# Selective scans beside other stages: work issued by its TensorE time, sums on four column tiles, wider rows of parts

## The chip, the cores and the metric

The kernel runs on one core of one Trainium2 chip. The metric is the device time of one execution in microseconds (us). The engines are named as in the profile: PE (TensorE), DVE (VectorE), ACT (ScalarE), POOL (GpSimd) and SP, the queue that issues nearly all DMAs.

## The reference

Four images of 96 channels and 64 x 64 pixels (L = 4096) pass through four residual layers, each on the group-normalised image (32 groups). All is float32.

```
layer 0: attention pooling: softmax over 4096 keys for 1024 queries, 3 heads of 32,
         a 3x3 neighbourhood softmax, a 5x5 depthwise convolution, a projection
layer 1: in_proj to 2 x 192 channels, 3x3 depthwise conv, silu, selective scan in four directions,
         layer norm, gate, 1x1 conv to 384, 3x3 depthwise conv, 1x1 conv to 96, squeeze-excite
layer 2: a dense 3x3 convolution
layer 3: 1x1 convs, two 3x3 depthwise branches, a selective scan like that of layer 1 (with D * u
         in place of layer 1's + D), layer norms, gates, squeeze convs, a channel softmax, a projection
scan, for each image, direction k, channel d (192) and state n (16), over 4096 positions t:
   delta = softplus(dt);  h[t] = exp(-delta[t] * A[d, n]) * h[t-1] + delta[t] * u[t] * B[n, t]
   y[t] = sum over n of h[t] * C[n, t]
directions: rows forward, rows backward, columns forward, columns backward; the four y are added
```

Layer 1's reference writes its recurrence as a ratio of cumulative sums; the kernel computes it as the recurrence above.

## The kernel before

A scan of one image in one layer is cut into 32 **groups**: four directions, four chunks of `CH` = 1024 positions, two halves of 96 channels. A group has `NG` = 12 **units**; a unit holds 8 channels x 16 states on 128 partitions and 1024 positions. Eight scans (`SCANS`: layer 1 of images 0 and 1, layer 3 of 0 and 1, then the same for images 2 and 3) make 3072 units, issued one after the other by `unit(i, ...)`.

What one unit does, by function:

- `fetch` (SP): a DMA spreads 8 rows of delta (`dd`, in DRAM) over 128 partitions into `rep`, 512 KB, four units ahead (`AHEAD`); `rep` has 10 buffers.
- `decays` (ACT): exp of `rep` times the decay rate, in place.
- `drive` (PE): two bf16 matmuls of 512 columns spread delta * u, which `prepare` cut into three bf16 parts (`parts`), over the 16 states into `bx`, a PSUM tile of two buffers.
- `times_b` (DVE): `bx` times B. `scan` (DVE): the recurrence as one instruction into `hs` (three buffers). `carry_on` (ACT) keeps the last column for the next chunk.
- `times_c` (POOL): `hs` times C, back into `rep`.
- `collect` (PE), every third unit: six float32 matmuls with 32 columns of weights (`addn`) add the 16 states of three units on three column tiles of the accumulator `acc` (PSUM, one buffer). `place` deals out the units so that each of the three tiles collects 32 channels in a row: rows 0 to 95 of `acc`.
- `output`, once a group: adds `acc` to `yo` or copies it (DVE or ACT), and SP stores it into `y_row` or `y_col` in DRAM, 96 rows. Backward directions first load what the forward ones left.

`prepare(g)` computes delta, delta * u, B and C of a group two groups ahead: a generator, advanced a step at a time in the slot `prep`. It writes du into DRAM and reads it back into `parts` by four DMAs of 24 partitions x 6 x 512 bf16 values.

**The other stages** run in the same stream. `first(b)` is layer 0 and the start of layer 1, `second(b)` the end of layer 1 to the start of layer 3's scan, `third(b)` the end of layer 3 and `last(b)` the same for the last image; `BESIDE` says which runs beside which scan (the last scan has `third` three times and `last`). `first(0)` runs ahead of the scans, alone. Each is a generator: it yields None after a matmul that something must evacuate, a number where only other engines have work, and a tuple inside a long accumulation. `Slots.begin` advances it up to such a point, `Slots.end` runs the evacuation.

Scheduling is by hand (`manual_schedule`): each engine runs its instructions in the order in which Python issues them. In `unit` the order was

```
first_.begin | decays(i+2) | scan(i) | carry_on(i-1) | times_c(i) | collect(j) | drive(i+2)
  | first_.end, rest.begin (if over 0.9 of the budget is left) | times_b(i+1) | output | first_.end, rest.end
```

where `first_` is a slot of work (or of `prep` in its first steps) and `rest` a second one. The budget is counted in yields: each matmul of a convolution is 1, an evacuated one 1, a number itself. A unit is given 3.5, 3.7 or 3.2 of it (`PACE`, by stage), less 2.1 where a `collect` is due, and what is left over is passed on (up to 0.5).

The names in profile lines: `one` and `held` are PSUM tiles of the other stages, `band`, `upad`, `vpad`, `hp` their padded images, `V` their working image, `ex` the attention's exponentials. All matmuls have one line, that of the helper `mm` (L949).

Of the kernel before, what the change touches and what calls it, by code (L numbers as in the profile page):

```python
# [18 lines left out]
L = H * W  # L19
# [21 lines left out]
PHI_EPS = 1e-12  # L41

# [101 lines left out]
def _constants(i):  # L144
    c = {}
    c["ident"] = np.eye(128, dtype=np.float32)
    g = np.zeros((128, 96), np.float32)
    for j in range(96):
        g[j // 3 * 3 : j // 3 * 3 + 3, j] = 1.0 / 3.0
    c["group"] = g  # L150
    c["ones"] = np.ones((128, 96), np.float32)
    c["mean1"] = np.full((128, 96), 1.0 / 96.0, np.float32)
    c["mean2"] = np.full((128, 96), 1.0 / 192.0, np.float32)


    s = np.zeros((128, 56), np.float32)
    s[np.arange(128), 24 + np.arange(128) % 8] = 1.0
    c["addn"] = s

    s = np.zeros((128, 2, 15), np.float32)  # L160
    s[:, 0, 7], s[:, 1, 7] = 1.0 / 96.0, 1.0 / 192.0
    c["means"] = s

    s = np.arange(34)[:, None] - np.arange(W)[None, :] // 2
    s = np.tile((s >= 0) & (s <= 2), (3, 2)).astype(np.float32)
    c["near"] = np.concatenate([s, np.zeros((26, 128), np.float32)])
    c["heads"] = np.kron(np.eye(4, dtype=np.float32), np.ones((32, 32), np.float32))

    s = np.zeros((2, 64, 4, E), np.float32)
    for tag, w in (("l1_", i["L1_conv_dt_proj_w"]), ("l3_", i["L3_conv_ss_dt_w"])):  # L170
        s[:, DTROW[tag] : DTROW[tag] + R] = w.transpose(2, 0, 1)
    c["dtw2"] = s.reshape(128, 4, E)

    for tag, w in (("l1_", i["L1_conv_A_log"]), ("l3_", i["L3_conv_ss_Alog"])):
        c[tag + "alogn"] = w.reshape(4, E // 8, 8, N).transpose(3, 2, 0, 1).reshape(128, 4, E // 8)

    s = np.zeros((4, 32, 4, N, 8), np.float32)
    for q in range(4):
        for d in range(8):
            s[q, 3 * d : 3 * d + 3, q, :, d] = 1.0  # L180
    c["spread"] = s.reshape(128, 4, 128)
    return c
# [712 lines left out]
def streams(ctx: ExitStack, tc: tile.TileContext, x, wts, cst, out, wat, cat, flag):  # L895
# [51 lines left out]

    def mm(o, lhsT, rhs, first=True, last=True):
        nc.tensor.matmul(o, lhsT=lhsT, rhs=rhs, start=first, stop=last)  # L949
# [58 lines left out]
    with tc.tile_pool(name="start", bufs=1) as T:  # L1008
# [9 lines left out]
        for tag in ("l1_", "l3_"):  # L1018
            decay[tag] = keep.tile([128, 4, E // 8], F32, name=tag + "decay")
            n, m, shape = cat[tag + "alogn"]  # L1020
            src = _view(t0, (n - n2, m, shape))
            if tag == "l3_":
                nc.scalar.activation(decay[tag], src, AF.Exp)
                src = decay[tag]
            nc.vector.tensor_scalar(decay[tag], src, -1.0, None, ALU.mult)
            dsum[tag] = derived(2)
            nc.vector.tensor_reduce(dsum[tag], wv(tag + "d"), AX.X, ALU.add)


    def image(name):  # L1030
        return [dram.tile([96, L], F32, name=f"{name}{b}") for b in range(B)]

    res1, res2, gate1, skip3, gate3 = (image(k) for k in ("res1_", "res2_", "gate1_", "skip3_", "gate3_"))
    u_row, u_col, y_row, y_col = ([image(f"{k}{h}_") for h in range(2)] for k in ("urow", "ucol", "yrow", "ycol"))
# [384 lines left out]
    def directions(pool, b, tag):  # L1419

        V = pool.tile([96, 2, L], F32, name="V", bufs=1)
        with tc.tile_pool(name="dirs", bufs=1) as T:
            full = len(groups) // len(SCANS) * (SCANS.index((tag, b)) + 1)
            cols = []
            for h in range(2):
                while stored[0] < full - 1 + h:
                    yield WAIT
                t = T.tile([96, W, H], F32, name="yc", bufs=2)
                cols.append(t)
                for j in range(4):  # L1430
                    nc.sync.dma_start(out=t.rearrange("p a b -> p (a b)")[:, bass.ts(j, CH)],
                                      in_=y_col[h][b][:, bass.ts(j, CH)])
                    nc.sync.dma_start(out=V[:, h, bass.ts(j, CH)], in_=y_row[h][b][:, bass.ts(j, CH)])
                yield 4
# [198 lines left out]
    def last(b):  # L1633

        with tc.tile_pool(name="p3x", bufs=1) as PX:
# [5 lines left out]
            with tc.tile_pool(name="turn", bufs=1) as T:  # L1641
                for h in range(2):
                    t = T.tile([96, W, H], F32, name="yc")
                    for j in range(4):
                        nc.sync.dma_start(out=t.rearrange("p a b -> p (a b)")[:, bass.ts(j, CH)],
                                          in_=y_col[h][b][:, bass.ts(j, CH)])
# [7 lines left out]
    def finish(PX, b, V, blocks):  # L1654

        with tc.tile_pool(name="p3", bufs=2) as pool:
# [25 lines left out]
            def loaded(name, src, bufs):  # L1682
                def load(j):
                    t = pool.tile([96, PCH], F32, tag=name, name=name, bufs=bufs)
                    nc.sync.dma_start(out=t, in_=src[b][:, bass.ts(j, PCH)])
# [126 lines left out]
    carry = keep.tile([128, 2, NG], F32, name="carry")  # L1812
    sums = keep.tile([96, len(SCANS), 4, 2, 2 * NCH], F32, name="sums")
    cuts = [keep.tile([128, 6, PCH], BF16, name=f"parts{n}") for n in range(2)]
# [24 lines left out]
    def prepare(g):  # L1839
# [83 lines left out]
        def to_parts():  # L1923
            for q in range(4):
                nc.sync.dma_start(
                    out=parts[32 * q : 32 * q + 24],
                    in_=du[:, :, bass.ts(q % 2, PCH)].rearrange("(s m d) r x -> m (d r) s x", m=2, d=8)[q // 2])
# [6 lines left out]
    def place(i):  # L1934
# [3 lines left out]
        return g, m % 3 * 4 + m // 3  # L1938

    def fetch(i):  # L1940

        g, m = place(i)
        rep = sp.tile([128, CH], F32, name="rep", bufs=10)
# [10 lines left out]
    def drive(i):  # L1954
# [4 lines left out]
        for e in range(2):  # L1959
            mm(bx[:, bass.ts(e, PCH)], spread[:, 2 * (m % 2) + e, :], parts[:, m // 2, :])  # L1960
# [25 lines left out]
    def collect(i):  # L1986
# [3 lines left out]
        if m == 0:  # L1990
            live["acc"] = ps.tile([128, CH], F32, tag="acc", name="acc", bufs=1)
            live["yo"] = sp.tile([96, CH], F32, name="yo", bufs=1)
            if back:
                nc.sync.dma_start(out=live["yo"], in_=(y_row if axis == "r" else y_col)[h][b][:, natural(c, back)])
            elif axis == "r" and tag == "l3_":
                nc.sync.dma_start(out=live["yo"], in_=u_row[h][b][:, natural(c, back)])
        hs = [live.pop(i + q)[0] for q in range(3)]
        w = addn[:, 24 - 8 * (m // 3) : 56 - 8 * (m // 3)]
        for e in range(2):
            for q in range(3):  # L2000
                mm(live["acc"][bass.ts(q, 32), bass.ts(e, PCH)], w, hs[q][:, bass.ts(e, PCH)], m == 0, m == NG - 3)

    def output(i):
# [4 lines left out]
        yo = live["yo"]  # L2008
        ya = time(live["acc"][:96], back, 0, CH)
# [13 lines left out]
    PACE = {"first": 3.5, "second": 3.7, "third": 3.2}  # L2023
# [15 lines left out]
    def unit(i, prep, work, budget):  # L2039
# [8 lines left out]
        j = i - BEHIND - 2  # L2048
        due = j >= 0 and j % 3 == 0
        first_, rest = (prep, work) if 1 <= prep.slots <= 3 else (work, idle)  # L2050
        budget -= first_.begin(budget)
# [5 lines left out]
        times_c(i)  # L2057
        if due:
# [3 lines left out]
        if first_ is work and budget > 0.9:  # L2062
            rest = work
        if rest is not idle:
            first_.end()
            budget -= rest.begin(budget)
        if i + 1 < total:
            times_b(i + 1)
        if due and j % NG == NG - 3:
            store.append(output(j))  # L2070
        first_.end()
        rest.end()
        if first_ is not prep:
            prep.begin(0)
            prep.end()
        return budget

    class Slots:
# [5 lines left out]
        def begin(self, budget):  # L2084

            if budget < 0:
                return 0
            self.slots += 1
            used = 0
            v = next(self.stage, 0)  # L2090
            if v == WAIT:
                return budget
            while isinstance(v, tuple):
                used += v[0]
                if used >= budget:
                    return used
                v = next(self.stage, 0)
            self.open = v is None
            return used + (1 if self.open else v)
# [19 lines left out]
    with tc.manual_schedule():  # L2119
# [15 lines left out]
        for i in range(total):  # L2135
# [11 lines left out]
            owed = min(owed, 0.5) + PACE[BESIDE[s][0][0]] - (2.1 if i % 3 == 1 else 0.0)  # L2147
            owed = unit(i, prep, work, owed)
        for j in range(total - 3, total, 3):
# [54 lines left out]
```

## Time and profile before

| | |
|---|---|
| three runs, median (lowest to highest) | 14,391.75 us (14,391.1 to 14,398.4) |
| the profiled execution, its own time | 14,400.5 us |
| its span, first to last instruction | 14,398.6 us |
| mean granted PE clock | 0.866 |
| PE / DVE / POOL / ACT busy | 84 / 81 / 71 / 61% |
| DMA: moved, mean rate | 2,644 MB, 184 GB/s |
| ahead of the first scan instruction | 690 us |
| the eight scans | 1632, 1656, 1666, 1633, 1630, 1659, 1668, 2036 us |
| after the last scan instruction | 129 us |

Busy shares are means over stages. In a group's line, the number after xcount is the busy time in us, then the mean duration in ns, then the idle time of the engine just ahead of it and what ended most of that. A waits line reads: who <- for whom: us in total, times, longest. float32 matmuls leave two records each.

### The profile page before, as it was taken

What the parts mean: (1) busy time and instruction counts of PE and PEld (TensorE: products, weight loads), DVE (VectorE), ACT (ScalarE), POOL (GpSimd) and SP (SyncE); (2) the same over time, 40 slices, a digit from 0 to 9 for tenths busy, and PEclk for the clock granted to TensorE, in tenths of its full rate; (3) what the DMA queues carried; (4) which work ended last, traced back from release to release, by engine and by line L of the source; (5) the groups of instructions that cost most, each with busy time, mean ns of one, the idle gap of its engine ahead of it and who ended that gap; (6) DMA issues with size and microseconds to landing.
All of it is one profiled execution on the core that took longest, in us unless ns stands there. A gap on an engine that the chain in (4) does not pass through costs nothing. (4 is left out here: it accounts for less than half of the span.)

```text
span 14398.6 us, 127507 instructions
## 1 busy us (share of the span) xinstructions
PE 12060.6 (84%) x40149; PEld 3562.9 (25%) x40802; DVE 11655.5 (81%) x7509; ACT 8713.8 (61%) x12340; POOL 10204.6 (71%) x4636
## 2 busy tenths in 40 slices
PE   8888887988889797889878887988979887777776
PEld 2322321322223222222222222222313222111111
DVE  1488898888878888889888898888888888778776
ACT  3266575557756676665766566566756667665554
POOL 0177886877868777778877787777868778666564
PEclk9889997998889897989879898898979888777777
DMA  0277787787877878778877788787877878677674
GB/s 9 64 174 179 193 216 198 187 207 187 223 178 199 205 200 209 180 174 206 223 185 178 186 209 219 176 207 186 212 186 197 209 190 220 168 179 173 161 184 111
DMA packets 902736, 2644.48 MB, mean 184 GB/s; under 512 B 107104, under 2 KB 257088, under 8 KB 902048
## 3 DMA queue, kind: packets, MB, share of 16 engines
q1 hardware_dynamic: 901392, 2634.72, 73.2%
q8 instruction: 324, 5.31, 0.2%
q14 instruction: 364, 2.98, 0.1%
q10 hardware_dynamic: 656, 1.46, 0.0%
HBM read 2169.16 MB, written 466.62 MB: 183 GB/s over the span
## 5 line engine op out<-in xcount | busy, mean ns | idle before, releaser
L1984 POOL TENSOR_TENSOR rep<-hs,bc 128x1024 f32<-128x1024 f32 x3072 | 7221.1, 2356 | 3057.2 <-DVE hs L1972 2499.8
L1972 DVE TENSOR_TENSOR_SCAN hs<-rep,carry,bx 128x1024 f32<-128x1024 f32 x2304 | 5401.7, 2344 | 266.0 <-ACT carry L1980 12.2
L1965 DVE TENSOR_TENSOR bx<-bx,bc 128x1024 f32<-128x1024 f32 x3072 | 3723.7, 1212 | 852.5 <-PE bx L949 432.9
L1952 ACT ACTIVATE rep<-rep,l_decay 128x1024 f32<-128x1024 f32 x3072 | 3495.7, 1143 | 519.9 <-DMA rep<-dd 502.7
L949 PE MATMUL bx<-parts,spread 128*128 128x512 bf16 x5491 | 1938.0, 429 | 1589.5 <-DVE hs L1972 1522.7
L949 PE MATMUL acc<-rep,ct 128*32 128x512 f32 x12288 | 2439.7, 703 | 16.0 <-POOL rep L1984 11.2
L1972 DVE TENSOR_TENSOR_SCAN hs<-rep,bx 128x1024 f32<-128x1024 f32 x768 | 1754.6, 2285 | 139.0 <-ACT carry L1980 47.8
L949 PEld LDWEIGHTS <-spread 128*128 128x128 bf16 x6144 | 426.0, 100 | 4080.5 <-DVE hs L1972 2610.9
L949 PE MATMUL one<-band,dg 96*96 96x512 f32 x2304 | 1048.0, 592 | 4.0
L949 PE MATMUL one<-upad,diag 96*96 96x512 f32 x2016 | 949.2, 607 | 3.8
L949 PEld LDWEIGHTS acc<-rep,ct 128*32 128x32 f32 x12288 | 492.2, 123 | 1676.0 <-issue 1401.2
L949 PE MATMUL one<-qq,kk 96*128 96x512 f32 x1152 | 684.4, 678 | 114.4 <-ACT ex L1288 75.2
L1288 ACT ACTIVATE ex<-one 128x512 f32<-128x512 f32 x576 | 342.4, 594 | 580.4 <-PE one L949 573.9
L949 PE MATMUL one<-pr,ct 6*96 6x512 f32 x1024 | 621.3, 690 | 78.6 <-DVE V L1193 10.4
L1952 ACT ACT_TABLE_LOAD x495 | 635.1, 1283 | 80.5 <-DMA rep<-dd 72.3
L949 PE MATMUL one<-hp,diag 96*96 96x512 f32 x1152 | 578.2, 642 | 31.3 <-POOL diag L1113 28.6
L1980 ACT COPY carry<-hs 128x1 f32<-128x1 f32 x2304 | 408.7, 177 | 287.0 <-DVE hs L1972 285.4
L949 PE MATMUL one<-vpad,diag 96*96 96x512 f32 x1200 | 559.2, 601 | 1.9
L949 PE MATMUL held<-ex,cols 128*32 128x256 f32 x3072 | 518.8, 415 | 8.0 <-ACT ex L1288 1.2
L949 PE MATMUL held<-ex,vT 128*32 128x256 f32 x3072 | 519.1, 415 | 0.0
L949 PEld LDWEIGHTS one<-band,dg 96*96 96x96 f32 x2304 | 374.6, 163 | 489.8 <-issue 423.7
L949 PEld LDWEIGHTS one<-upad,diag 96*96 96x96 f32 x2016 | 336.7, 167 | 438.9 <-issue 378.2
(3421 smaller groups left out, 14154.2 us busy)
## 6 DMA issues: line engine op xcount, KB each, us to landing
rep<-dd SPq DMA_DIRECT2D x3072, 512.0 KB
parts<-du SPq DMA_DIRECT2D x1024, 144.0 KB
bc<-rows SPq DMA_DIRECT2D x256, 512.0 KB
dd<-delta SPq DMA_DIRECT2D x256, 384.0 KB
du<-cut SPq DMA_DIRECT2D x256, 384.0 KB
us<-urow SPq DMA_DIRECT2D x128, 384.0 KB
du<-cut SPq DMA_DIRECT2D x256, 192.0 KB
yrow<-yo SPq DMA_DIRECT2D x128, 384.0 KB
```

Of the source, the lines that this page charges most:

```text
L949: nc.tensor.matmul(o, lhsT=lhsT, rhs=rhs, start=first, stop=last)
L1288: nc.scalar.activation(last.rearrange("p a b -> p (a b)"), p, AF.Exp, scale=HD**-0.5)
L1952: nc.scalar.activation(a, a, AF.Exp, scale=decay[tag][:, k, NG * h + m : NG * h + m + 1])
L1965: nc.vector.tensor_mul(bx, bx, ready[i // NG][2][:, 0, :])
L1972: nc.vector.tensor_tensor_scan(out=hs, data0=a, data1=bx, initial=carry[:, h, m : m + 1] if c else 0.0, op0=ALU.mult, op1=ALU.add)
L1980: nc.scalar.copy(carry[:, h, m : m + 1], live[i][1][:, CH - 1 : CH])
L1984: nc.gpsimd.tensor_tensor(a, hs, ready[i // NG][2][:, 1, :], ALU.mult)
```

## The change

1. **Issue by PE time.** `mm` adds up an estimate of PE time (`spent`: columns x passes / 2400; bf16 one pass, float32 four, 32-column tiles 1.07, the two-tile product of `prepare` two). A unit is given `PACE[s]` us (2.95 to 3.45 by scan), less `DRIVE` 0.43 and, where a `collect` is due, `SUM` 1.71; up to 0.6 is passed on. A step without matmul counts `SLOT` 0.5 per number.
2. **Order in the unit.** Work is issued in up to three portions: ahead of the scan, ahead of `collect` and `drive`, and after `drive`. `times_b(i+1)` moves up to just after `times_c(i)`; all evacuations come after it.
3. **Four units a sum.** `collect` takes four units on four column tiles, one unit later (`BEHIND - 3`); `place` is `m % 4 * 3 + m // 4`. Each 32 partitions of `acc` hold 24 channels and a gap of 8, so `yo`, `y_row` and `y_col` have 128 rows, `yo` is one lasting tile, the sum of D (`dsum`) comes from a constant in that layout, and the other stages read y without the gaps by four DMAs of 24 rows each (`ungapped`).
4. **Parts** are [128, 3, 1024]: four DMAs of 24 partitions x 3 x 1024 values, rows of 2048 bytes; `drive` picks one of four row blocks and half of the columns.
5. `rep` has 12 buffers[...].

The diff, cut to its core:

```
+PACE = (2.95,3.45,3.45,2.95,2.95,3.45,3.45,3.2)
...
     def mm(o, lhsT, rhs, first=True, last=True):
+        n = 1
+        for d in rhs.shape[1:]:
+            n *= d
+        m = o.shape[0]
+        passes = 1 if rhs.dtype == BF16 else 1.07 if m == 32 else 2 if m == R + 2 * N else 4
+        spent[0] += n * passes / 2400
...
+    def ungapped(dst, src, cols):
+        for q in range(4):
+            nc.sync.dma_start(out=dst[24 * q : 24 * q + 24], in_=src[32 * q : 32 * q + 24, cols])
...
-                    nc.sync.dma_start(out=t.rearrange("p a b -> p (a b)")[:, bass.ts(j, CH)],
-                                      in_=y_col[h][b][:, bass.ts(j, CH)])
-                    nc.sync.dma_start(out=V[:, h, bass.ts(j, CH)], in_=y_row[h][b][:, bass.ts(j, CH)])
+                    ungapped(t.rearrange("p a b -> p (a b)")[:, bass.ts(j, CH)], y_col[h][b], bass.ts(j, CH))
+                    ungapped(V[:, h, bass.ts(j, CH)], y_row[h][b], bass.ts(j, CH))
...
-                    in_=du[:, :, bass.ts(q % 2, PCH)].rearrange("(s m d) r x -> m (d r) s x", m=2, d=8)[q // 2])
+                    in_=du.rearrange("(s m d) r x -> m (d r) s x", m=4, d=8)[q])
...
-        return g, m % 3 * 4 + m // 3
+        return g, m % 4 * 3 + m // 4
...
-        rep = sp.tile([128, CH], F32, name="rep", bufs=10)
+        rep = sp.tile([128, CH], F32, name="rep", bufs=12)
...
-            mm(bx[:, bass.ts(e, PCH)], spread[:, 2 * (m % 2) + e, :], parts[:, m // 2, :])
+            mm(bx[:, bass.ts(e, PCH)], spread[:, m % 4, :], parts[:, m // 4, bass.ts(e, PCH)])
...
-        hs = [live.pop(i + q)[0] for q in range(3)]
-        w = addn[:, 24 - 8 * (m // 3) : 56 - 8 * (m // 3)]
+        hs = [live.pop(i + q)[0] for q in range(4)]
+        w = addn[:, 24 - 8 * (m // 4) : 56 - 8 * (m // 4)]
         for e in range(2):
-            for q in range(3):
-                mm(live["acc"][bass.ts(q, 32), bass.ts(e, PCH)], w, hs[q][:, bass.ts(e, PCH)], m == 0, m == NG - 3)
+            for q in range(4):
+                mm(live["acc"][bass.ts(q, 32), bass.ts(e, PCH)], w, hs[q][:, bass.ts(e, PCH)], m == 0, m == NG - 4)
...
-    PACE = {"first": 3.5, "second": 3.7, "third": 3.2}
+    DRIVE, SUM, SLOT = 0.43, 1.71, 0.5
...
-        j = i - BEHIND - 2
-        due = j >= 0 and j % 3 == 0
-        first_, rest = (prep, work) if 1 <= prep.slots <= 3 else (work, idle)
-        budget -= first_.begin(budget)
+        j = i - BEHIND - 3
+        due = j >= 0 and j % 4 == 0
+        left = budget - DRIVE - (SUM if due else 0.0)
+        mine = 1 <= prep.slots <= 3
+        left -= prep.begin(1.0) if mine else work.begin(left)
         if i + 2 < total:
             decays(i + 2)
         scan(i)
         if i:
             carry_on(i - 1)
         times_c(i)
+        if i + 1 < total:
+            times_b(i + 1)
+        if mine:
+            prep.end()
+        work.end()
+        left -= work.begin(left)
         if due:
             collect(j)
         if i + 2 < total:
             drive(i + 2)
-        if first_ is work and budget > 0.9:
-            rest = work
-        if rest is not idle:
-            first_.end()
-            budget -= rest.begin(budget)
-        if i + 1 < total:
-            times_b(i + 1)
-        if due and j % NG == NG - 3:
+        work.end()
+        left -= work.begin(left)
+        if due and j % NG == NG - 4:
             store.append(output(j))
-        first_.end()
-        rest.end()
-        if first_ is not prep:
-            prep.begin(0)
+        work.end()
+        if not mine:
+            prep.begin(1.0)
             prep.end()
-        return budget
+        return left
...
-            used = 0
+            t = spent[0]
...
             while isinstance(v, tuple):
-                used += v[0]
-                if used >= budget:
-                    return used
+                if spent[0] - t + 0.4 > left:
+                    return spent[0] - t
                 v = next(self.stage, 0)
             self.open = v is None
-            return used + (1 if self.open else v)
+            return max(spent[0] - t, SLOT * (1 if self.open else v))
...
-            owed = min(owed, 0.5) + PACE[BESIDE[s][0][0]] - (2.1 if i % 3 == 1 else 0.0)
+            owed = min(owed, 0.6) + PACE[s]
...
-    nc = bacc.Bacc("TRN2", target_bir_lowering=False, num_devices=1)
+    nc = bacc.Bacc("TRN2", target_bir_lowering=False, num_devices=1,
+                   dynamic_dma_scratch_size=1024)
```

## The prediction

> **What bounds the kernel now.** I read the page from the top: shares by engine, then the costliest groups, then a table of stretches cut at the starts of the eight scans (the first and last scan instruction of each give the cuts), then DVE's waits within the scans.
>
> ```profile
> PE 12060.6 (84%) x40149; PEld 3562.9 (25%) x40802; DVE 11655.5 (81%) x7509; ACT 8713.8 (61%) x12340; POOL 10204.6 (71%) x4636
> ...
> L1972 DVE TENSOR_TENSOR_SCAN hs<-rep,carry,bx 128x1024 f32<-128x1024 f32 x2304 | 5401.7, 2344 | 266.0 <-ACT carry L1980 12.2
> L1965 DVE TENSOR_TENSOR bx<-bx,bc 128x1024 f32<-128x1024 f32 x3072 | 3723.7, 1212 | 852.5 <-PE bx L949 432.9
> ...
> L949 PE MATMUL acc<-rep,ct 128*32 128x512 f32 x12288 | 2439.7, 703 | 16.0 <-POOL rep L1984 11.2
> ```
>
> No engine is full. The third and fourth lines are what every unit must do on DVE: 2.34 + 1.21 us. Where nothing waits, the timeline has two scans 3.60 us apart (6640.42, 6644.02, 6647.62), so 3072 units cannot take less than 3072 x 3.604 = 11,071 us.
>
> ```profile
> 2322.00:3978.00 1656.00, 1423.67 (x4256) 427.90 (x4332) 1403.94 (x870) 1057.22 (x1454) 1268.59 (x571) 0.89 0.79 198
> ...
> 5644.00:7277.00 1633.00, 1380.93 (x5474) 415.39 (x5568) 1410.53 (x860) 1017.26 (x1479) 1273.58 (x573) 0.87 0.79 196
> ...
> 12234.00:14270.00 2036.00, 1518.63 (x3855) 364.75 (x3922) 1596.51 (x1133) 1205.30 (x1699) 1267.59 (x593) 0.76 0.69 171
> ```
>
> Columns: stretch, us, busy PE, PEld, DVE, ACT, POOL, granted clock, DMA share, GB/s. These are scans beside `second`, `first` and `third`. The eight scans take 13,580 us (690 to 14,270). DVE is busy 11,444 us of them; 10,880 is the scan and its multiply, so 564 us is DVE work of the other stages. Floor 11,071 + 564 = 11,635; the excess, **1,945 us of stalls**, is all that a better order can win. What stalls DVE:
>
> ```profile
> DVE bx L1965 <- PE bx L949: 432.9, 281, 11.8
> DVE bx L1965 <- PE acc L949: 350.4, 175, 8.0
> DVE yo L2011 <- PE acc L949: 159.9, 77, 6.6
> DVE V L1193 <- PE one L949: 118.0, 48, 9.9
> DVE x L1600 <- ACT one L1599: 100.3, 32, 6.9
> ```
>
> Three classes. **Late drive**: 783 us in which `times_b` waits because PE, in order, has other work or a `collect` ahead of the unit's two `bx` matmuls. **Late sums**: 160 + 55 us (the L2017 line) in which the output waits for `acc`. **Late evacuation**: DVE reads another stage's matmul (L1193, L1600 and some twenty smaller lines), some 640 us together. The same order costs PE: it waits 1,523 us with its `bx` matmul for the scan to release PSUM (view of waits, PE bx <- DVE hs), while work that could have run stands behind it.
>
> [...]12 records of 703 ns mean would be 8.4 us in a row, and the sums took 2439.7 / 1024 = 2.38 us of PE per `collect`. [...]2590 to 2781, PE busy 190 of 191 us, ran at 1.00; the `third` scan, busy 75%, at 0.76. [...]
>
> **The change part by part.**
>
> *Four column tiles.* 768 sums of eight matmuls replace 1024 of six. If four tiles take the time of three, PE is spared 256 x 2.38 = 609 us, some 76 us a scan. At worst four take 4/3 as long and nothing is spared. I take the first. Hardly any of it is on the path by itself; it counts through the next item.
>
> *Equal shares.* I counted the matmul time issued between consecutive drives in both orders of instructions[...] (512 f32 columns 0.85 us; the trace spaces such weight loads 2 x 0.43 us at full clock). Before, 1,166 units hold more than 3.6 us and 505 more than 4.5; after, 880 and 133. At the granted 0.866, a unit holds its time without a stall up to 3.6 x 0.866 = 3.12 us; the larger of 3.12 and the unit's work, summed and divided by 0.866, is 12,967 us before and 12,048 after: 918 us less. That is an upper estimate, because PE may run up to about 3 us late before DVE feels it, so part of the 918 is no stall today. I take 55% of the two classes it can touch, late drive and late sums (998 us): **-550 us** (bounds -250 and -800). Next in line there is the output itself, which still needs its last `collect` in the same unit.
>
> *Order within the unit.* Before, the second portion of work stood behind `drive(i+2)`, hence behind the end of the scan, and the first portion's evacuation mostly stood ahead of `times_b`. The timeline at 12,454 shows it: drive 12454.82, `one<-xz` 12455.26, ACT after, DVE L1729 at 12456.11 after 1.35 us of waiting, and only then `times_b` at 12456.77. Of these portions 1,079 end in an evacuation. After, 893 second portions stand ahead of `collect` and `drive`, 301 third ones behind, and all evacuations come after `times_b`. The third ones still stall, so I take a bit over half of the 640 us: **-350 us** (-100 to -500).
>
> *SP.* The y images have 128 rows with gaps, so a load is four DMAs of 24 rows. The order of instructions has 504 more DMAs; at 0.42 us each (median of yc<-ycol) 212 us of SP, of which 8 to 32 loads in one unit matter: at 2340 the present eight take 5.0 us and the next `rep` fetch follows. With 32 it is 13.4 us[...]. The fetches run four units (14.4 us) ahead, so most of it is covered where nothing else is late, but this place already stalls (scans 7.1, 10.9 and 9.4 us apart from 2341). Two bursts in seven scans, some 4 us each: **+60 us** (0 to +150). Stores and reloads of 128 rows add a third to 384 transfers of 384 KB, 50 MB to 2,644.
>
> *At nothing:* parts' rows of 2048 bytes. 147,456 packets of 94 ns become 73,728 of about 106 ns, 380 us of sixteen engines; DMA is 0.69 to 0.79 busy, and waits of ACT for `rep` (503 us) reach the scan as 7 us only. If the tighter scans make DMA the bound, this is the cover. Two more `rep` buffers free the fetch one unit earlier at the same lead: also only cover. 33 fewer table loads (1.28 us) lie on ACT, 61% busy. The `yo` on 128 partitions, `d` as a constant, and the smaller descriptor scratch cost nothing that a row shows (DVE's and ACT's time goes by the 1024 columns).
>
> Sum: -550 - 350 + 60 = -840 us on the profiled 14,400.5 us (span 14,398.6). The median of the three runs is 9 us below that, so 14,392 - 840 = **13,550 us**.
>
> **The rivals.**
>
> *The chain is the bound (little gain).* Beside `third`, layer norm, gate and squeeze run PE, ACT, DVE in turn, and DVE's share is 78% with PE's 75%: no equal shares shorten a chain. For it: that scan alone has 2036 - 384 x 3.604 - 236 (DVE's 1,596 less 384 x 3.54) = 416 us of stalls. Against: more than half the stalls stand in the other scans, on `bx`. A third of my gain: -280, 14,110 us.
>
> *PE held up by its own portions (slower).* The second portion now stands ahead of `collect` and `drive`. Where it needs the first portion's evacuation (relu, then the next matmul), PE waits for ACT, 0.6 to 0.8 us and 1.28 for a table, or for DVE after scan and multiply; the drive behind it is late, and every stage hangs on it. 893 such portions. The gain is gone at 840 / 893 = 0.94 us each. At 1.3 us the time is 14,392 - 840 + 1,160 = 14,710 us. Against: the ACT evacuation can end before the scan does, and up to 3 us of lateness are free.
>
> *Both classes all but vanish.* PE busy more evenly brings the clock towards 1.0, and 1,945 us of stalls lose two thirds: 14,392 - 1,300 = 13,090 us. For it: from 1664 to 1709, beside convolutions of 25 taps without a chain, twelve units already take 45 us.
>
> **How the numbers follow.** My forecast (13,200 to 13,900) 0.55, both vanish 0.15, little gain (13,900 to 14,360) 0.16, slower 0.12, no change 0.02 (within 0.2%, 29 us, about what a measurement can tell). The range 13,000 to 14,180 cuts off the best of the third rival, the top of the first and all of the slower one, some 0.2. Faster 0.86, same 0.02, slower 0.12.
>
> **What would show it.** Right: scans beside `first` and `second` of 1,520 to 1,570 us and the last near 1,800; `times_b` waiting for PE under 400 us; `acc` busy near 1,830 us; a higher granted clock in the scans; PE's wait for `hs` shorter. Wrong: `acc` still at 2,400; PE waiting for ACT with `one` ahead of `bx`; ACT waiting for `rep` or `yc` at scan starts much above 500 us, which would make the bursts the cost; scans unchanged with stalls moved from `bx` to `V` and `x`.

## The result, and the profile after

| | median (lowest to highest) | ratio to the kernel before | 95% interval |
|---|---|---|---|
| before | 14,392.16 us (14,391.1 to 14,398.4) | 1 | |
| after | 14,256.25 us (14,250.58 to 14,277.47) | 0.9907 | 0.989 to 0.9925 |

The change makes the kernel 136 us (0.9%) faster, where 840 us were forecast; the time lies above the range. The profiled execution of after has a span of 14,248.7 us and a mean granted clock of 0.859 (before 14,398.6 and 0.866).

The page of after: shares by engine, then the two DVE groups that every unit runs, and the sums.

```profile
PE 11588.7 (81%) x40137; PEld 3442.3 (24%) x40802; DVE 11635.9 (82%) x7509; ACT 8680.4 (61%) x12307; POOL 10197.3 (72%) x4637
...
L1996 DVE TENSOR_TENSOR_SCAN hs<-rep,carry,bx 128x1024 f32<-128x1024 f32 x2304 | 5401.2, 2344 | 301.6 <-ACT carry L2004 33.3
L1989 DVE TENSOR_TENSOR bx<-bx,bc 128x1024 f32<-128x1024 f32 x3072 | 3720.1, 1211 | 862.4 <-PE bx L964 616.7
...
L964 PE MATMUL acc<-rep,ct 128*32 128x512 f32 x12288 | 1833.1, 712 | 11.8 <-POOL rep L2008 8.7
```

The sums fell from 2,440 to 1,833 us, as forecast: 1833.1 / 768 = 2.39 us a `collect` of eight matmuls, against 2.38 us of six. But the idle time ahead of `times_b` (the second group) is 862 us where it was 853.

DVE's waits:

```profile
DVE bx L1989 <- PE bx L964: 616.7, 313, 17.4
...
DVE yo L2035 <- PE acc L964: 106.0, 52, 20.6
DVE bx L1989 <- PE acc L964: 99.6, 60, 10.9
DVE x L1620 <- ACT one L1619: 92.0, 28, 7.7
...
DVE bx L1989 <- PE one L964: 78.3, 65, 5.7
DVE V L1214 <- PE one L964: 72.2, 44, 5.9
...
DVE bx L1989 <- remote: 60.8, 15, 30.2
```

`times_b` waited for PE 433 + 350 + 7 = 790 us before, and 617 + 100 + 78 = 795 us after. Whether such a wait is named `bx`, `acc` or `one` says nothing of what was late: the traces of before and after hold 5,491 and 5,479 of the 6,144 matmul records of the drive, and of the waits named `acc`, `one` or "remote" (no releaser found, 54 us before and 61 after) nearly all before and nine in ten after belong to units with one drive record missing. That goes for the prediction's split of its late drives too; their sum stands. In the runs whose traces hold all 6,144 every such wait is named `bx`. So runs are compared below by the whole idle time ahead of `times_b`, from the pages. The waits of the output for `acc` fell from 160 + 55 to 106 + 19 us (the smaller lines are L2017 and L2041). DVE's waits in the other stages (its lines without `bx`, `hs`, `yo` and the attention's `rs` and `top`) fell from 774 to 700 us in sum. The gain stands in these two.

The stretches cut at the starts of the scans (us, busy PE, PEld, DVE, ACT, POOL, granted clock, DMA share, GB/s), the same three as before:

```profile
2351.00:3997.00 1646.00, 1370.64 (x4254) 419.15 (x4332) 1400.96 (x869) 1053.69 (x1449) 1267.30 (x571) 0.87 0.81 203
...
5627.00:7231.00 1604.00, 1298.84 (x5472) 391.51 (x5568) 1409.55 (x860) 1012.84 (x1476) 1272.83 (x573) 0.89 0.81 203
...
12078.00:14119.00 2041.00, 1474.40 (x3859) 350.85 (x3930) 1594.20 (x1132) 1180.57 (x1679) 1265.06 (x593) 0.74 0.69 174
```

They took 1,656, 1,633 and 2,036 us before: 10 and 29 us won, 5 lost. Of the five others, the first scan lost 29 us (1,632 to 1,661) and four won 35 to 40. PE was spared 53 and 82 us of busy time in the first two lines above and its share *fell* from 86 to 83% and from 85 to 81%: most of the time it was spared became idle time.

Inside one scan, beside `second` of image 0, three stretches of 48 units show what became of the gain. Before:

```profile
2590.00:2781.00 191.00, 190.38 (x605) 64.50 (x614) 168.49 (x97) 119.53 (x163) 155.15 (x68) 1.00 0.78 194
2781.00:2975.00 194.00, 192.43 (x606) 64.46 (x616) 169.83 (x100) 115.50 (x179) 157.19 (x69) 1.00 0.81 200
3183.00:3388.00 205.00, 166.03 (x497) 47.48 (x504) 173.78 (x109) 133.77 (x204) 158.18 (x69) 0.88 0.76 188
```

After, the same units:

```profile
2617.00:2792.00 175.00, 172.53 (x579) 59.15 (x589) 167.25 (x97) 117.14 (x161) 156.78 (x69) 1.00 0.87 215
2792.00:2972.00 180.00, 175.11 (x580) 59.24 (x590) 169.34 (x100) 115.70 (x176) 156.89 (x69) 0.99 0.91 224
3186.00:3411.00 225.00, 179.46 (x537) 53.34 (x545) 173.84 (x112) 142.97 (x214) 158.03 (x70) 0.87 0.69 174
```

The first two lie beside a dense convolution, where matmuls wait for nothing: PE was full, and 30 us were won, down to 175 and 180 us where 48 x 3.604 = 173 is the floor. The third lies beside `x -> r -> l_lin -> hp`, where each matmul needs an evacuation of the one before. It **lost** 20 us at a PE share of 80%. The units are the same, the work beside them is not quite: the dense stretches hold 26 matmul records fewer each than before and this one 40 more, so the even budgets moved work into it.

What such a loss looks like, in the timeline of after, engine by engine (start, us, instruction, in brackets the idle time just before it and what ended it). PE:

```profile
3287.65 1.91 PE L964 MATMUL one<-X,l_c 96*96 96x512 f32 x2
3294.22 2.02 PE L964 MATMUL one<-r,l_lin 96*96 96x512 f32 x2 [4.66 <-ACT r L1591]
3296.18 2.82 PE L964 MATMUL acc<-rep,ct 128*32 128x512 f32 x16
3298.93 0.39 PE L964 MATMUL bx<-parts,spread 128*128 128x512 bf16 x1
...
3302.01 1.10 PE L964 MATMUL one<-r,l_lin 96*96 96x512 f32 x2 [1.62 <-ACT r L1591]
```

ACT beside it:

```profile
3287.90 0.69 ACT L1596 ACTIVATE hp<-one,wt 96x512 f32<-96x512 f32 x1 [2.11 <-PE one L964]
3288.60 1.28 ACT L1918 ACT_TABLE_LOAD   x1
3289.89 1.06 ACT L1918 ACTIVATE w__16251<-w__16251 96x1024 f32<-96x1024 f32 x1
3290.97 1.28 ACT L1976 ACT_TABLE_LOAD   x1
3292.26 1.15 ACT L1976 ACTIVATE rep<-rep,l_decay 128x1024 f32<-128x1024 f32 x1
3293.32 0.17 ACT L2004 COPY carry<-hs 128x1 f32<-128x1 f32 x1
3293.40 0.77 ACT L1591 ACTIVATE r<-one,der 96x512 f32<-96x512 f32 x1
```

And DVE:

```profile
3286.36 2.35 DVE L1996 TENSOR_TENSOR_SCAN hs<-rep,carry,bx 128x1024 f32<-128x1024 f32 x1
3299.57 1.23 DVE L1989 TENSOR_TENSOR bx<-bx,bc 128x1024 f32<-128x1024 f32 x1 [10.86 <-PE acc L964]
```

Read it from the end: DVE waits 10.86 us with `times_b` for the drive at 3298.93 (one of its two records is missing, so the line names the sums just ahead). The drive is behind a `collect` and a matmul of `l_lin`, PE waits 4.66 us with that one for `r`, and ACT has `r` behind `hp`, a step of `prepare`, two table loads of 1.28 us, `rep` and `carry`. In these 4.66 us PE is idle, because an instruction that isn't ready stands ahead of the drive. What PE does next is slow as well: the granted clock is 0.50 until 3298.04, so the pair of `l_lin` takes 2.02 us, where the next pair, at 1.00, takes 1.10.

Over the whole run, the lines of PE's waits with `one` sum to 716 us for ACT (before 408) and 292 us for DVE (before 49), while its wait for `hs` went down (before 1,522.7):

```profile
PE bx L964 <- DVE hs L1996: 1123.4, 752, 12.8
PE one L964 <- ACT yt L1458: 183.3, 64, 13.8
PE one L964 <- ACT ex L1309: 137.3, 146, 3.3
...
PE one L964 <- ACT r L1591: 52.2, 27, 5.4
```

What did PE do while `times_b` waited? The traces' records of PE and of its clock, which hold only 1.0 and 0.5, split its waits of over 60 ns as follows (us). The last row is a run of nearly the same time as the changed kernel, whose trace lacks no record of the drive.

| kernel | waits | PE busy at full clock | at half clock | PE idle |
|---|---|---|---|---|
| before | 822 | 504 | 279 | 39 |
| tiles, gaps, parts alone | 852 | 485 | 310 | 57 |
| second portion behind drive | 851 | 357 | 434 | 60 |
| changed kernel | 832 | 293 | 420 | 118 |
| evacuations ahead of `times_b` | 791 | 278 | 425 | 88 |

The part in which PE simply had too much to do went down by 211 us from before to after. In its place came 141 us of matmuls at half clock and 79 us in which PE itself waits (by the last row, up to 30 us of these may be missing records).

### The profile page after: what moved, and what is told of

It is laid out like the page before. It is cut to its first block, busy times and chain, and to the rows that moved or that the text cites. A ratio compares the mean times of both kernels' runs of the same rounds, so it can differ in the third digit from the quotient of the medians.

```text
span 14248.7 us, 127656 instructions
## 1 busy us (share of the span) xinstructions
PE 11588.7 (81%) x40137; PEld 3442.3 (24%) x40802; DVE 11635.9 (82%) x7509; ACT 8680.4 (61%) x12307; POOL 10197.3 (72%) x4637
## 4 chain that ended last, share of the span: by engine, by line
PE 36%; DVE 20%; ACT 15%; DMA 11%; issue 7%; POOL 7%; SPq 1%; DVEq 0%; POOLq 0%; ACTq 0%
PE one L964 24%; DVE hs L1996 12%; PE bx L964 6%; PE acc L964 6%; DVE bx L1989 6%; DMA rep<-dd 5%; ACT rep L1976 4%; POOL rep L2008 4%; ACT L1976 1%; DMA du<-cut 1%; PE held L964 1%; ACT ex L1309 1%; DMA parts<-du 1%; DMA yc<-ycol 1%; ACT L1918 1%
## 5 line engine op out<-in xcount | busy, mean ns | idle before, releaser
L964 PE MATMUL acc<-rep,ct 128*32 128x512 f32 x12288 | 1833.1, 712 | 11.8 <-POOL rep L2008 8.7
L964 PEld LDWEIGHTS <-spread 128*128 128x128 bf16 x6144 | 458.6, 102 | 3655.5 <-DVE hs L1996 2239.6
L964 PE MATMUL one<-pr,ct 6*96 6x512 f32 x1024 | 691.3, 761 | 69.9 <-ACT pr L1881 24.6
L964 PEld LDWEIGHTS acc<-rep,ct 128*32 128x32 f32 x12288 | 374.3, 123 | 1268.0 <-issue 1026.3
```

## The experiments

Differences in us below are (ratio - 1) x 14,392, so that runs of different jobs can be set side by side; their intervals are some 25 us to either side, and some 35 us where two of them are subtracted.

| kernel | median, us | ratio, 95% interval | against before |
|---|---|---|---|
| changed kernel | 14,256 | 0.9907 (0.989 to 0.9925) | -134 |
| second portion behind drive | 14,665 | 1.0213 (1.0191 to 1.0236) | +307 |
| tiles, gaps, parts alone | 14,678 | 1.0211 (1.0194 to 1.0228) | +304 |
| issue alone | 14,287 | 0.9941 (0.9924 to 0.9957) | -85 |
| loads in fours alone | 14,455 | 1.0054 (1.0034 to 1.0073) | +78 |
| evacuations ahead of `times_b` | 14,260 | 0.991 (0.9893 to 0.9928) | -130 |
| two fillers | 14,497 | 1.0073 (1.0054 to 1.0092) | +105 |
| four fillers | 14,914 | 1.0363 (1.0344 to 1.0381) | +522 |
| tiles alone, two fillers | 14,897 | 1.035 (1.033 to 1.0369) | +504 |
| tiles alone, same density | 14,556 | 1.0113 (1.0097 to 1.013) | +163 |
| whole loads | 14,321 | 0.9953 (0.9936 to 0.9969) | -68 |
| chained portions behind drive | 14,216 | 0.9874 (0.9858 to 0.9891) | -181 |
| and no third one at sums | 14,180 | 0.9865 (0.9846 to 0.9884) | -194 |
| chained behind, loads spread | 14,209 | 0.9877 (0.9862 to 0.9892) | -177 |
| chained behind, three tiles | 14,265 | 0.9919 (0.9906 to 0.9933) | -117 |

### The parts of the change

**The second portion behind drive.** The changed kernel with

```
-        left -= work.begin(left)
         if due:
             collect(j)
         if i + 2 < total:
             drive(i + 2)
+        left -= work.begin(left)
         work.end()
```

> The changed kernel with one move: the second portion of work is issued behind collect and drive instead of ahead of them. Theory A (PE is held up by its own portions: the second portion's matmul waits for the first's evacuation and keeps collect and drive behind it): PE's waits of `one` for ACT, DVE and DMA fall from some 1,200 us towards the 520 us of the kernel before, times_b's wait for PE falls from 800 to under 600, and the time from 14,256 to 13,980 to 14,150 us. Theory B (the y loads in fours at SP eat the gain): no change, 14,220 to 14,290. Theory C (stages that are chains; the portions' place only moves the stall from times_b to the evacuations): 14,240 to 14,400.

It is 441 us slower than the changed kernel, outside all three forecasts. That moving the whole second portion helps is refuted. PE's waits with `one` for ACT and DVE did fall (1,008 to 719 us), and its wait with `bx` for `hs` rose from 1,123 to 1,632 us: ahead of drive, the portion fills time in which PE waits for the scan. The idle time ahead of `times_b` is hardly longer (882 against 862 us); what is longer is DVE's waits in the other stages, 972 us against 700. Equal shares and four tiles with the later portions all behind drive are a loss of 307 us.

**Tiles alone**: the changed kernel with `unit`, `Slots` and the budgets of before, and `- (2.1 if i % 4 == 1 else 0.0)`.

> The changed kernel's tiles, gaps, rows of parts and buffers with the budgets and the order of the kernel before (2.1 off where a sum of four is due). Theory A: the tiles spare 600 us of PE of which a third or so was in the way: 14,100 to 14,300, as fast as the whole change or faster. Theory B: the loads in fours cost what the tiles spare: 14,350 to 14,500. Theory C: 14,250 to 14,350, the tiles are all that the change brings.

Slower than any of the three. The tiles with the old issue lose 304 us, and with the budgets by PE time but the second portion behind drive, as above, 307: between these two, equal shares (with `times_b` and the evacuations moved) bring nothing.

**Issue alone**: the kernel before with the budgets, `spent`, `unit` and `Slots` of after; three tiles, y images of 96 rows, old parts.

> The kernel before with the new budgets by PE time and the new order in the unit; sums of three units, y of 96 rows, loads as before. Theory A: the even shares gain in the convolutions and the order loses in the stages with chains: 14,330 to 14,550. Theory B: the gain without the loads' cost: 13,900 to 14,150. Theory C: 14,350 to 14,450.

Between theories A and B.

**Loads in fours alone**: the kernel before, its y loads cut into four.

```
+    def quarters(dst, src, cols):
+        for q in range(4):
+            nc.sync.dma_start(out=dst[24 * q : 24 * q + 24], in_=src[24 * q : 24 * q + 24, cols])
```

> The kernel before with each load of y by the other stages cut into four DMAs of 24 rows, nothing else. Theory A and C: a small cost at the starts of seven scans, 14,400 to 14,480. Theory B: 14,600 to 14,900, enough to hide a gain of some hundred us in the change.

Issue alone wins 85 us, tiles alone lose 304, together they win 134: the tiles are worth -49 us on top of the new issue and +304 on top of the old. The loads alone, on the kernel before, cost 78 us, as theories A and C had it. If they cost the same with the tiles, what else the tiles bring is about -127 us with the new issue and +226 with the old.

**The density of issue.** In tiles alone, 2.1 is taken off one unit in four instead of one in three, so a unit is given 2.1 x (1/3 - 1/4) = 0.175 more. With the budgets lowered:

```
-    PACE = {"first": 3.5, "second": 3.7, "third": 3.2}
+    PACE = {"first": 3.325, "second": 3.525, "third": 3.025}
```

> Four column tiles, gaps, wider rows of parts and twelve rep buffers with the budgets and the order in the unit of before, as in the run of the tiles alone (14,678 us), but with 0.175 less in every budget (3.325, 3.525, 3.025), so that a unit is given as much on the average as before: there the 2.1 is taken off one unit in four instead of one in three, which gave 0.175 more. Theory E (the 290 us that the tiles lost alone are a matter of how densely the other stages' work is issued, plus the 77 us of the loads in fours): 14,400 to 14,500 us, times_b's waits for PE back under 800 us. Theory T (the tiles or the wider rows cost something by themselves, with the budgets of before): 14,600 to 14,700, about the same as the run of the tiles alone. In between: both.

In between: 141 of the 304 us go; with the 78 of the loads some 85 us are left without a cause of their own. The 0.175 a unit that the rarer deduction gave to the other stages cost 141 us, although the sums had spared PE about 0.2 us a unit (609 / 3072). Why it costs so much is not shown.

### Is PE's load, or its clock, the lever?

The changed kernel with matmuls that change nothing, ahead of drive in eight units of twelve:

```
+        if i >= 5 and (i % NG >= 5 or i % NG == 0):
+            for e in range(2):
+                nc.tensor.matmul(live["acc"][:, bass.ts(e % 2, PCH)], lhsT=null,
+                                 rhs=spread.rearrange("p a b -> p (a b)"), start=False, stop=False)
```

`null` is a tile of zeros; the four fillers have `range(4)`, and the same two were put into tiles alone.

> The changed kernel with two bf16 filler matmuls of 512 columns (weights zero, added to acc, so nothing is left out) ahead of the drive in 8 of 12 units: 2 x 0.21 us of PE work at full clock, 870 us in all. Theory D (the clock[...]): the half-clock time in the scans falls from 3,860 us to under 3,000 and the kernel is as fast or faster, 14,050 to 14,280. Theory E (PE's load counts, whatever the clock): each filler stands ahead of the drive and the time rises by a third to all of 870 us: 14,500 to 15,100.

> The same with four fillers, 1,740 us of PE work at full clock. Theory D: clock near 0.95, half-clock time under 2,000 us; time within 150 us of that with two, PE being full in the dense stages only. Theory E: 15,000 to 15,900.

> The kernel with the tiles alone (budgets and order of the kernel before; 14,678 us) and two fillers a unit, about the 600 us of PE time that the four-unit sums spare. Theory D: most of the loss against the kernel before comes back, 14,400 to 14,560, with half-clock time from 4,659 us to under 3,900. Theory E: slower still, 14,850 to 15,400.

The page with two fillers:

```profile
PE 12310.8 (85%) x44896; PEld 3815.8 (26%) x44896; DVE 11674.0 (81%) x7509; ACT 8677.5 (60%) x12307; POOL 10203.5 (70%) x4638
...
L964 PE MATMUL acc<-rep,ct 128*32 128x512 f32 x12288 | 1767.1, 689 | 4.7 <-POOL rep L2010 4.7
L2095 PE MATMUL acc<-spread,null 128*128 128x512 bf16 x4094 | 1320.2, 406 | 0.0
```

Tiles alone lost 200 us more by the same two. The granted clock rose from 0.859 to 0.885 and 0.909, the time at half clock in the scans fell from 3,860 to 3,185 and 2,543 us (with tiles alone from 4,659 to 3,725), and the kernel got slower each time: theory D is refuted, and the numbers of theory E are met with tiles alone and missed from below, by 3 and 86 us, in the other two. A higher clock bought with work ahead of the drive doesn't pay. Whether it would pay if nothing stood ahead of the drive for it was not tried: a filler brings load and clock together, and the table above has half clock in 420 of the 832 us. PE's busy time rose by 722 us for 239 us of time, 0.33 us a us; from two fillers to four it rose by 610 us (the page with four has 12,921.0) for 417 us, 0.68 a us. These prices are for us of busy time on balance: the two fillers themselves were busy 1,320 us, and all other matmuls, at the higher granted clock, 598 us less than without them. By them PE's load is a third on the path here, and more where there is more of it.

### The order in the unit

**Evacuations ahead of `times_b`**: the changed kernel with the two lines of `times_b(i + 1)` moved behind `prep.end()` and `work.end()`.

> The changed kernel with the first portion's evacuation ahead of times_b instead of after it (its second portion then follows later too). If the place of the evacuations was worth the 350 us that the prediction gave it: 14,450 to 14,700. If it is worth little, as DVE's evacuation waits (683 us before, 611 after) say: 14,220 to 14,350.

No difference (0.991 against 0.9907), as the second number had it.

**Chained portions behind drive.** The changed kernel with

```
+        chained = work.open
         work.end()
-        left -= work.begin(left)
+        if not chained:
+            left -= work.begin(left)
         if due:
```

> The changed kernel, but the second portion stands ahead of collect and drive only where the first portion of the unit ended without an evacuation; where it ended with one, the next portion comes behind drive. Theory P (in chains the second portion makes PE wait for the evacuation of the first ahead of the unit's drive, and this gives back in the chain stages what the convolutions win): faster than the changed kernel by 60 to 200 us, 14,060 to 14,200, PE's waits with one for ACT well under 737 us, and times_b's waits for PE under 600. Theory Q (a portion ahead of drive fills time in which PE waits for the scan anyhow, in chains too, and moving it behind drive moves the stall to the next unit): slower, 14,350 to 14,660; the upper end is the run that moved all second portions behind drive (14,665).

47 us faster than the changed kernel: theory P as to the direction, but short of its 60 us, and `times_b`'s waits are above its 600. PE's waits with `one` went from 716 to 577 us for ACT and from 292 to 205 for DVE, the idle time ahead of `times_b` from 862 to 728; PE waits for `hs` again instead (1,340 us), and the output more for `acc` (125 to 195 us). The two lines, of DVE's waits and of PE's:

```profile
DVE bx L1989 <- PE bx L964: 724.6, 384, 30.0
...
PE bx L964 <- DVE hs L1996: 1340.3, 847, 10.9
```

So the portions ahead of drive that depend on nothing are worth 488 us there (307 + 181, against having all behind), and the dependent ones cost 47.

**And nothing behind drive in a unit with sums and a chained portion**: in the same kernel,

```
         work.end()
-        left -= work.begin(left)
+        if not (due and chained):
+            left -= work.begin(left)
         if due and j % NG == NG - 4:
```

> As the run that moved chained portions behind drive (14,216 us), and in a unit with a collect whose first portion ended with an evacuation nothing more is issued behind drive: such a unit gives PE at most one portion of a chain beside the sums. times_b's waits stand mostly behind acc there (217 of 688 us with PE busy on acc) and behind other work (206). Theory P carried on (what is left of the late drives comes from two dependent portions in a unit that also has the sums): 14,130 to 14,190 us. Theory R (the chain's length sets the time: what isn't issued here stalls in a later unit): 14,200 to 14,300; the work is as much and ends within 20 units of the scan's end in either.

0.9865 against 0.9874 of the run before: inside both intervals, so theory P carried on is not shown, though its median lies within that theory's numbers and is the lowest of all, below both kernels. The idle time ahead of `times_b` is 716 us against 728.

**Three tiles under that rule**: issue alone, with `chained` as above.

> The issue part alone (three column tiles, y images of 96 rows, narrow rows of parts, ten rep buffers; 14,287 us) with the rule that a second portion stands ahead of collect and drive only where the first ended without an evacuation. Theory P (chained portions hold up drive whatever the tiles are): faster than the issue part alone by 30 to 100 us, 14,190 to 14,260. If four tiles are worth their 609 us of PE at the price that the fillers showed (0.28 a us, 170 us) less the 77 us of the loads, this stays some 30 to 90 us above 14,216: 14,245 to 14,305. If it is at 14,216 or below, the tiles and the wider rows bring nothing in any order of issue.

117 us below before, 32 us faster than issue alone (within the interval of such a difference), 64 us short of the same rule with four tiles. So tiles and wide parts are worth 64 us here and 49 without the rule; with the 78 us that their loads cost, if they cost it here too, 142 and 127. If all of that is due to the 609 us of PE that four tiles spare, and none to the wider rows and the buffers, which were not run apart, some 0.22 us a us reach the end.

### The loads

**Whole loads**: the changed kernel, four DMAs of 24 x 4096 for each image instead of sixteen of 24 x 1024.

```
-                for j in range(4):
-                    ungapped(t.rearrange("p a b -> p (a b)")[:, bass.ts(j, CH)], y_col[h][b], bass.ts(j, CH))
-                    ungapped(V[:, h, bass.ts(j, CH)], y_row[h][b], bass.ts(j, CH))
+                ungapped(t.rearrange("p a b -> p (a b)"), y_col[h][b], bass.ts(0, L))
+                ungapped(V[:, h, :], y_row[h][b], bass.ts(0, L))
```

> The changed kernel, with the loads at the start of second and third over the whole image: four DMAs of 24 rows by 4096 columns for each image of y instead of sixteen by 1024 columns, so 8 DMAs in the burst instead of 32, the same bytes and the same 24 rows to a DMA. The loads in fours cost 77 us on the kernel before. If SP's time for issuing 32 DMAs ahead of the next rep fetch is the price, this wins 40 to 80 us: 14,180 to 14,215. If it is the 24 rows[...], it wins nothing: 14,240 to 14,270, and may lose a little where the first piece of the stage now waits for its whole image instead of a quarter of it.

**Loads spread** over four steps (the `yield 4` behind the loop becomes `yield 1` inside), on the kernel with chained portions behind drive:

> As the run that moved chained portions behind drive (14,216 us), with the y loads at the start of second and third spread over four steps (8 DMAs of 24 rows and one step, four times, for each image) instead of 32 in one step. The loads in fours cost the kernel before 77 us, and loads of whole images (8 DMAs, same bytes) cost the changed kernel 65 us more, so the number of DMAs is not the price. Theory B (the burst of 3 MB ahead of the next rep fetches is the price): 14,120 to 14,170 us, the first 48 units of scans 1 and 7 shorter by 5 to 15 us each. Theory G (the first use waits for its own data[...]): 14,200 to 14,230 or slower, since the last loads now come later.

Whole loads cost 66 us with a quarter of the DMAs, slower than either forecast. PE's waits name a likely cause, one that this run brought with it: the first matmul on `V` now waits for the whole image instead of a quarter, a line that was 10.8 us in the changed kernel:

```profile
PE one L964 <- DMA V<-yrow: 114.4, 7, 22.7
```

So this run doesn't tell whether SP's time for issuing 32 DMAs is the price: a gain of 40 us could hide behind these waits. Spreading them changes nothing (0.9877 against 0.9874), as theory G had it, though ACT, which turns the loaded columns, waits less for them; its waits before spreading:

```profile
ACT yt L1458 <- DMA yc<-ycol: 51.8, 5, 11.0
ACT yt L1458 <- DMA V<-yrow: 31.7, 2, 17.2
```

and after:

```profile
ACT yt L1458 <- DMA yc<-ycol: 15.1, 5, 12.1
ACT yt L1458 <- DMA V<-yrow: 4.9, 2, 4.5
```

64 us of waiting for data went, and no time: theory B's gain did not come, and that wait was not what set the end. Whether the 24 rows of a DMA are a price is not shown either: no view here shows the DMA engines singly. That the 78 us are real is shown by the loads in fours alone; by which wait they reach the end stays open. The loads of `last`, which have the same four DMAs, were not varied apart.

## Why the prediction was wrong

**Four column tiles: right.** 1,833 us of sums for 1,830 forecast. Their worth was left to the next item.

**Equal shares, -550 us: the step that failed.** It was the larger of 3.12 us and a unit's matmul time, divided by the clock of the mean, so it had no term for a matmul that isn't ready, and it held the clock constant. On top of the tiles, with the second portion left behind drive, the new budgets brought nothing to speak of (+304 us to +307), and from before to after the two classes that the step was to halve went from 998 to 920 us (795 + 106 + 19). What it did price right is the overload: PE busy at full clock while `times_b` waits fell from 504 to 293 us, and in the dense stretches 191 and 194 became 175 and 180 us. What took its place are the two things left out: matmuls at half clock, 279 to 420 us, and PE waiting itself, 39 to 118. PE's waits with `one` for ACT and DVE rose from 457 to 1,008 us over the run (408 + 49 to 716 + 292). Their sum is not their price: they fell to 719 us in the run that was 441 us slower, and the portions that depend on the one before cost 47. How the rest of the missing gain divides between waits and clock is not shown. The mean clock went down, not towards 1.0: 0.866 to 0.859. A us of PE spared brought some 0.22 us, and one added cost 0.33 to 0.68.

**Order in the unit, -350 us: a fifth of it.** DVE's waits in the other stages, of which the step took a bit over half, fell by 74 us. Of its two parts, the evacuations behind `times_b` are worth nothing. The second portion ahead of drive is worth 441 us, but against the new budgets and tiles with it behind drive, where these waits are 972 us and not the 774 of before: most of it only makes good what the rest of the change loses.

Both together were forecast at -900 us; issue alone, which is both without the PE time of the tiles, measured -85 (-109 to -62).

**SP, +60 us: right in size** (+78), but the 4 us a burst were the author's estimate and no run shows them, so the number may be luck.

**At nothing:** ACT's wait for `rep` rose from 503 to 852 us, above the 500 named as a sign against. The fetches wait less for a buffer (SP's wait `rep` <- PE `acc`, 2,575 to 611 us), but the store of du now waits ahead of them (L1944 for ACT's `cut`, 294 to 1,290 us). That is not the whole account: tiles alone has the store's wait too (1,352 us) and 612 us at `rep`, issue alone has not (354) and 698 us. The scan's own wait for ACT's `rep` is a line of 12.7 us, so little of it reaches DVE that way; no run took the rows of parts or the buffers alone.

**The rivals.** "The chain is the bound" came nearest (14,110 us). The stretch that lost time shows its mechanism beside `second`; beside `third`, for which it was put forward, the scan went from 2,036 to 2,041 us. "PE held up by its own portions" was real where a portion depends on the one before, but at 47 us, not 1,160: its count of 893 portions put all of them on one side, and those that depend on nothing are worth 488. "Both classes all but vanish" needed a clock towards 1.0, which did not come. Of the signs named for being right, the sums' 1,830 us and PE's shorter wait for `hs` came; of those for being wrong, PE waiting for ACT with `one` ahead of `bx`, and ACT's longer wait for `rep`.

Open are the 85 us that tiles lose with the old issue beyond loads and density, the way in which the loads cost 78 us, why the denser issue cost 141 us, and what would bring the idle time ahead of `times_b` well below the 716 us of the best version. It moved the time less than it moved itself: 862 to 716 us, 76 us of median.

## What to carry to other kernels

Ahead of an instruction on the critical path of an in-order engine, put work that is ready, and keep behind it work that depends on something just issued: the second portion was worth 441 us in that place on the whole, and cost 47 where it depended on the one before. A model of the time that sums an engine's durations priced the dense stretches here well and the chains not at all, so split a stage by whether its matmuls wait for an evacuation before taking a gain from evening them out. When an operation on such an engine becomes shorter, tune the budgets around it anew: here the old rule turned the shorter sums into 141 us of loss. And before reading a wait by the name of its releaser, count the records of what should have ended it.

## What the runs showed of the hardware

At a granted clock of 1.00 the two bf16 matmuls of a drive, 512 columns each, took 0.43 us together, and a float32 matmul of 512 columns 0.86 us (before: a drive starts at 2602.23, the next matmul at 2602.66, and four of these later the next drive at 2606.10). Eight float32 matmuls of 512 columns on four column tiles took as long as six on three (2.39 and 2.38 us). DVE's add of `acc` to `yo`, 1024 columns, took 1.22 us on 96 partitions (before) and on 128 (after), ACT's copy 1.00 us on both. The clock records of these traces hold only 1.0 and 0.5, and the same pair of matmuls took 1.10 us at the one and 2.02 us at the other. With two and four fillers the mean granted clock was 0.885 and 0.909 where it was 0.859 without, and the time was 239 and 656 us longer all the same: 0.33 us for each us that the first two added to PE's busy time on balance, 0.68 for each that the next two added.
